# Leaving the last projection steps of a block's end to run beside the next end, in a four-layer sparse attention kernel

## The chip, the core and the metric

The kernel runs on one core of one Trainium2 chip. The metric is the device time of one execution in microseconds. The engines are called PE (matrix multiply), DVE (vector), ACT (scalar), POOL (GpSimd) and SP (the queue that issues plain DMAs). Each takes its own instructions in the order in which the program wrote them, and waits on semaphores for the others.

## What is computed

Sixteen graphs share one adjacency matrix of 1024 nodes; every node has 128 features. Four layers follow each other. Layers 0, 2 and 3 are attention over the neighbours with 8 heads, followed by a normalization, a feed-forward net of width 256 and another normalization; layer 1 is a simpler graph attention with one head. The matrix is sparse (a bit under 1 % of its entries are set), so the kernel gathers each node's neighbours instead of multiplying full matrices.

```python
# layers 0, 2, 3
Q, K, V = h @ Wq, h @ Wk, h @ Wv                # 8 heads of 16
attn = softmax(where(adj == 0, -inf, Q K^T / 4))
x = layer_norm(h + (attn @ V) @ Wo + bo)
x = layer_norm(x + relu(x @ W1 + b1) @ W2 + b2)
# layer 1
h = x @ W;  e = leaky_relu(h @ a_src + (h @ a_dst)^T)
x = layer_norm(softmax(where(adj == 0, -inf, e)) @ h + x)
```

## The kernel before

**Blocks and parts.** The work is a list of 64 blocks (`units`): 4 layers, 2 halves of 8 graphs (`g`), 8 tiles of 128 nodes (`t`). A block is gone through in parts, each of which gathers up to two chunks of neighbour rows (four in layer 1) by indirect DMAs on POOL's queue. A block of an attention layer has five parts (seven for tile 0), a block of layer 1 has three (four for tile 0). Here the five parts of a block are called A, B, C, D and E; E is the half-size mixed chunk. A prime marks the next block's parts.

**One turn of the main loop** (line 1055) handles part i in this order: `products(i)` on DVE (line 868); `summed(i-2)`, the PE sums of weighted rows (line 935); a gap; `exponentials(i)`, a DVE reduction (line 891) and an ACT exponential (line 895); a gap; `weighted(i-1)` on DVE (line 919); `gathered(i+3)`, the indirect DMAs on POOL (line 856), into one of four buffers; a gap. In layer 1 there are four gaps in a turn. The products live in four buffers, and `weighted` writes over the products of its part. A buffer is free again when `summed` has read it. Two parts that belong together are summed at once: A with B when D's turn comes, C with D in the turn of A', E in the turn of B'.

**The end of a block.** When a block's last part is summed, `divided(u)` computes the denominators on PE (the den step) and, later in the same turn, runs its second half: a DVE reciprocal (line 972), two DVE products that write `o` (line 975), an ACT copy and a POOL addition into `seen` (line 986). That point is called the closing here; it falls in the turn of the next block's part B. It creates two generators, the block's tails, one for each set of four graphs (h = 0 and h = 1). A tail is a chain of small steps:

oT (transpose of `o`, line 637), Wo (line 644), squares (line 580, ACT), power (line 586, POOL), scale (line 589, ACT), x1 (transpose, line 650), W1 with its two relus (lines 655 and 659), W2 (line 664), squares, power, scale, turn (transpose of the normalized rows, line 614), projection p0, projection p2 (line 538 on PE, line 542 on ACT), and the write of the table for the next layer (line 547, SP).

The tail of h = 1 is one step behind. The last layer has no projection: its steps after turn are a second transpose and an indirect DMA to `out` (line 625, POOL). A tail of layer 1 is shorter, because it has one normalization and no feed-forward net.

**Where the steps run.** `others()` is called in every gap. A counter (`pace`) decides whether the gap advances all tails by one step, and then one step of the next block's queries is taken (lines 799 to 832: Wq, then the replication of the queries). The rate is set at the closing: 15 steps (8 for layer 1) spread over the gaps up to the next closing. Before the second half of `divided`, all tails that are left are run to their end, `while tails: advance(tails)`. So in the kernel before, a tail always ends within one opening, the stretch from one closing to the next. With 15 steps in an opening, only the last step of h = 1, the issue of its table write, is left for that loop or the last gap.

**Buffers that tie the tails to the closing.** `o` and the normalized rows `z` share one tag with two buffers. The tile `o` of a half can only be written when the turn of the same half of the previous end has read its `z`. The small banks of PSUM (tag `ps`) are four, `yps` two.

Of the kernel before, what the change touches and what calls it, by code (L numbers as in the profile page):

```python
# [107 lines left out]

STEPS = 15
GRAPH_STEPS = 8  # L110
EDGES = 4
AHEAD = 4

# [9 lines left out]
def sparse_path(ctx: ExitStack, tc: tile.TileContext, a: dict, out: bass.AP, flag):  # L123
# [48 lines left out]
    inputs = ctx.enter_context(tc.tile_pool(name="inputs", bufs=4))  # L172
    gathers = ctx.enter_context(tc.tile_pool(name="gathers", bufs=EDGES))
    reps = ctx.enter_context(tc.tile_pool(name="reps", bufs=2))
# [7 lines left out]
    def gather_buffer():  # L182
        return gathers.tile([P, max(4 * ROW, J * (ROW + G))], F32, tag="e", name="e")
# [408 lines left out]
    def turned(z, dst, gain=None, shift=None):  # L592

        ps = bank([P, GH, P])
        for i in range(GH):
            nc.tensor.transpose(ps[:, i, :], z[:, i, :], ident)  # L596
        if gain is None:
            nc.scalar.copy(dst, ps)  # L598
        else:
            nc.scalar.activation(dst, ps, AF.Identity, bias=shift, scale=gain)  # L600
# [4 lines left out]
    def finish(l, g, t, h, z, gain, shift):  # L605
        if l + 1 < len(LAYERS):

            wanted[0] = True
            while held[0]:
                advance(slow)  # L610
            wanted[0] = False
            busy[0] += 1
            xn = states.tile([P, GH, P], F32, tag="xT", name="xT")
            turned(z, xn, gain, shift)
            yield
            yield from project(l + 1, g, t, h, xn)
            busy[0] -= 1
            return
        xn = states.tile([P, GH, P], F32, tag="xT", name="xT")
        turned(z, xn, gain, shift)  # L620
        yield
        o = twos.tile([P, GH, D], F32, tag="kv", name="outs")
        turned(xn, o)
        yield
        nc.gpsimd.indirect_dma_start(  # L625
            out=out.rearrange("n (k c) -> (n k) c", k=GR * HF),
            out_offset=bass.IndirectOffsetOnAxis(ap=places[:, g, h, t : t + 1], axis=0),
            in_=o.rearrange("p g d -> p (g d)"), in_offset=None,
        )

    def attention_tail(l, g, t, h, o):
# [38 lines left out]
        z = yield from normed(ps)  # L670
        yield
        yield from finish(l, g, t, h, z, p["ln2_g"], p["ln2_b"])

    def graph_tail(l, g, t, h, o):
# [53 lines left out]
    def at_once(g):  # L728

        spare = reps.tile([P, J, ROW], F32, tag="qr", name="spare")  # L730

        def fetch(t):
            if t < T:
                nc.sync.dma_start(
                    spare[:, t % J, :], a["x"][t * P : (t + 1) * P, columns(g, 0, HF)]
                )

        for t in range(3):
            fetch(t)
        yield  # L740
        for t in range(T):
            fetch(t + 3)
            rows = spare[:, t % J, :].rearrange("p (h g d) -> p h g d", h=HF, g=GH)
            both = []
            for h in range(HF):
                kv = None
                if h:
                    kv = exponents()[:, : 2 * GH * D].rearrange("p (c g d) -> p c g d", c=2, g=GH)
                both.append(natural(g, t, h, rows[:, h], kv))
            while both:  # L750
                advance(both)
                yield
# [5 lines left out]
    units = [(l, g, t) for l in range(len(LAYERS)) for g in range(GR) for t in range(T)]  # L758
# [10 lines left out]
    def is_attention(u):  # L769
        return LAYERS[units[u][0]][1] is ATTN  # L770
# [93 lines left out]
    def products(i):  # L864
        u, (piece,) = parts[i]
        n = len(piece)
        prs[i] = [prods.tile([P, 2, ROW], F32, tag="pr", name="pr")]
        nc.vector.tensor_tensor(  # L868
            prs[i][0][:, :n, :], es[i][:, :n, :ROW],
            qx[u].rearrange("p (o c) -> p o c", o=1) if (MIX, 0) in piece  # L870
            else of_piece(qs[u], piece),
            ALU.mult,
        )
# [114 lines left out]
    tails = []  # L988
    fronts = []
    loads = []  # L990
    slow = []

    def advance(gens):
        for gen in list(gens):
            if next(gen, "end") == "end":
                gens.remove(gen)

    pace = [0.0, 0.0]

# [17 lines left out]
    with tc.manual_schedule():  # L1017
        wide = [gather_buffer() for _ in range(EDGES)]
        setup, entry, weights = graph(wide), at_once(0), load_weights("L0")
        next(setup)  # L1020
        next(weights)
        next(entry)
        more = [weights, load_graph_weights()]
        rest = slots()
        for i, room in enumerate(setup):
            if i == T:
                for gen in more:
                    next(gen)
            if room == "load":
                for _ in loaded(0):  # L1030
                    next(entry, None)
            elif room == "queries":
                for _ in entry:
                    pass
                for _ in queries(0):
                    pass
            elif isinstance(room, str):
                next(rest)
            else:
                for _ in range(room):  # L1040
                    next(entry, None)
        for _ in entry:
            pass
        scratch.close()
        prods = ctx.enter_context(tc.tile_pool(name="prods", bufs=4))
        smalls = ctx.enter_context(tc.tile_pool(name="smalls", bufs=3))
        slow.append(at_leisure(1))
        for i in range(AHEAD - 1):
            gathered(i)
        nc.gpsimd.memset(wide[3], 0.0)  # L1050
        gathered(AHEAD - 1)
        fronts.extend([rest, loaded(1)] + more)
        closing = None
        begun = 0
        for i in range(len(parts) + 2):
            here = i < len(parts)
            u = parts[i][0] if here else len(units)
            if here:
                l = units[u][0]
                if i and parts[i - 1][0] != u:  # L1060
                    begun = i
                    if l + 1 < len(LAYERS) and LAYERS[l + 1][1] is ATTN:
                        if units[u][1:] == (0, 1):
                            more = load_weights(LAYERS[l + 1][0])
                            next(more)
                            next(more)
                        if units[u][1:] == (0, 4):
                            next(more, None)
                if is_attention(u):
                    products(i)  # L1070
            if i > 1:
                summed(i - 2)
                done = parts[i - 2][0]
                if parts[i - 1 : i] == [] or parts[i - 1][0] != done:
                    closing = divided(done)
                    next(closing)
            others()
            if here:
                exponentials(i)
            if here and i == begun + 1:  # L1080
                if is_attention(u):
                    shared(u)
                while loads:
                    advance(loads)
                if u + 1 < len(units):
                    fronts.append(queries(u + 1))
                loads.append(loaded(u + 2))
                if units[u + 2 : u + 3] and units[u + 2][0]:
                    advance(loads)
            others()  # L1090
            if 0 < i <= len(parts):
                weighted(i - 1, 0)
                if not is_attention(parts[i - 1][0]):
                    others()
                    weighted(i - 1, 2)
                gathered(i - 1 + AHEAD)
            if closing is not None and here:
                while tails:
                    advance(tails)
                for _ in closing:  # L1100
                    pass
                closing = None
                passes = 3 if is_attention(u) else 4
                steps = STEPS if is_attention(done) else GRAPH_STEPS
                pace[:] = 0.0, steps / (passes * sum(part[0] == u for part in parts) - 1)
            others()
            if i + 1 >= len(parts) or parts[i + 1][0] != u:

                while fronts:
                    advance(fronts)  # L1110
        while tails:
            advance(tails)
        for _ in closing:
            pass
        while tails:
            advance(tails)
# [434 lines left out]
```

## Time and profile before

| | |
|---|---|
| time, median of 14 runs | 2545.02 us (2532.22 to 2552.59) |
| the profiled execution | 2552.59 us, span 2550.8 us |
| mean granted PE clock | 0.909 |
| DVE busy | 1930.8 us (76 %) |
| PE busy | 2107.0 us (83 %) |
| ACT busy | 1475.2 us (58 %) |
| POOL busy | 1431.0 us (56 %) |
| start of the closings of layer 0, first and last | 190.1 us, 849.0 us |
| of layer 1 | 889.3 us, 1193.6 us |
| of layer 2 | 1240.2 us, 1846.3 us |
| of layer 3 | 1892.3 us, 2508.1 us |

The shares are means over layers with different limits, so the profile is read layer by layer and, within a layer, over one opening. A regular opening takes about 41 us in layer 0, 19 us in layer 1, 39 us in layer 2 and 41 us in layer 3. In a timeline, each row gives the start, the duration, the engine, the line, the operation, the tiles, and in brackets the idle time of that engine just before and what ended it.

### The profile page before, as it was taken

Reading aid. Unit: us, or ns where it says so; the run is one execution under the profiler, and the core shown is the slowest. Engines: PE = TensorE matmul, PEld = TensorE weight load, DVE = VectorE, ACT = ScalarE, POOL = GpSimd, SP = SyncE. Lnnn points to the kernel's source line nnn. Section 1 sums busy time; section 2 is a strip of 40 time slices with the busy share of each in tenths; the row PEclk is TensorE's granted clock in tenths of the full one; section 3 lists DMA queues with packets and bytes.
Section 4 is the critical chain, followed back from the end, with each engine's and each line's share of the span. In section 5 each row is a group of like instructions: output and inputs, shape, how many; then the busy total and the mean of one; then the engine's idle time right before and its main releaser. Section 6 shows DMA issues by size and latency. Waiting matters only on the chain. (4 is left out here: it accounts for less than half of the span.)

```text
span 2550.8 us, 36646 instructions
## 1 busy us (share of the span) xinstructions
PE 2107.0 (83%) x13124; PEld 1305.5 (51%) x13124; DVE 1930.8 (76%) x1470; ACT 1475.2 (58%) x4640; POOL 1431.0 (56%) x978
## 2 busy tenths in 40 slices
PE   6558898788887998998888888888988787788787
PEld 5425666545554554554455555655555454455444
DVE  7887787587878466676887879878797877888781
ACT  3216776566655554455476656667666565566565
POOL 3234656356665588884545546455555665665561
PEclk8679999898898999998799999999999898989898
DMA  7646888567777598897877877878777667566750
GB/s 249 236 164 225 294 289 286 208 232 251 239 253 246 167 329 317 301 340 257 277 261 247 295 260 264 276 266 287 267 259 264 238 230 264 196 231 238 244 208 19
DMA packets 168461, 636.05 MB, mean 249 GB/s; under 512 B 38328, under 2 KB 41144, under 8 KB 119774
## 3 DMA queue, kind: packets, MB, share of 16 engines
q0 software_dynamic: 92672, 485.09, 54.3%
q1 hardware_dynamic: 75600, 148.55, 17.3%
q8 instruction: 105, 1.72, 0.3%
q14 instruction: 84, 0.69, 0.1%
HBM read 603.11 MB, written 92.34 MB: 273 GB/s over the span
## 5 line engine op out<-in xcount | busy, mean ns | idle before, releaser
L856 POOL DMA_INDIRECT e<-table,idx x600 | 917.4, 1529 | 458.5 <-DVE pr L919 260.3
L919 DVE TENSOR_TENSOR pr<-e,ex 128x2048 f32<-128x2048 f32 (+1 forms) x336 | 689.6, 2060 | 203.2 <-ACT ex L895 174.8
L868 DVE TENSOR_TENSOR pr<-e,qr 128x2048 f32<-128x2048 f32 x204 | 460.9, 2259 | 180.4 <-PE acc L935 83.1
L586 POOL TENSOR_TENSOR rstd<-total,power 128x4 f32<-128x4 f32 x224 | 325.6, 1456 | 394.2 <-ACT z L580 387.0
L935 PE MATMUL acc<-pr,marks 128*32 128x512 f32 x2656 | 498.1, 620 | 39.8 <-DVE pr L919 39.3
L891 DVE TENSOR_REDUCE sc<-pr 128x128 f32<-128x2048 f32 (+1 forms) x252 | 518.5, 2058 | 8.6
L580 ACT ACTIVATE z<-yps,root 128x128 f32<-128x128 f32 x896 | 318.5, 378 | 99.6 <-PE yps L683 51.8
L596 PE MATMUL ps<-ident,z 128*128 128x128 f32 x896 | 212.6, 338 | 151.5 <-ACT z L589 151.3
L589 ACT ACTIVATE z<-yps,rstd 128x128 f32<-128x128 f32 x896 | 257.7, 383 | 92.9 <-POOL rstd L586 92.5
L596 PEld LDWEIGHTS ps<-ident,z 128*128 128x128 f32 x896 | 136.3, 159 | 335.8 <-ACT z L589 242.0
L659 ACT ACTIVATE f<-ps,b 128x512 f32<-128x512 f32 x192 | 131.9, 690 | 277.3 <-PE ps L655 277.3
L655 PE MATMUL ps<-x,W 128*128 128x512 f32 x384 | 252.0, 791 | 37.4 <-ACT x L600 37.4
L664 PE MATMUL yps<-W,f 128*128 128x128 f32 x1536 | 259.1, 286 | 17.1 <-ACT f L659 15.9
L664 PEld LDWEIGHTS yps<-W,f 128*128 128x128 f32 x1536 | 211.2, 195 | 77.7 <-ACT f L659 59.0
L935 PEld LDWEIGHTS acc<-pr,marks 128*32 128x32 f32 x2656 | 102.2, 112 | 285.3 <-issue 223.1
L538 PE MATMUL ps<-Wkv,xT 128*128 128x256 f32 x768 | 207.2, 414 | 32.4 <-ACT xT L600 27.6
L831 ACT COPY qr<-ps 128x512 f32<-128x512 f32 x384 | 197.0, 600 | 61.8 <-PE ps L828 61.8
L580 ACT ACTIVATION_READ_ACCUMULATOR z<-yps,root 128x1 f32 x896 | 194.1, 217 | 0.0
L538 PEld LDWEIGHTS ps<-Wkv,xT 128*128 128x128 f32 x768 | 146.0, 201 | 72.3 <-ACT xT L600 34.1
L542 ACT COPY kv<-ps 128x512 f32<-128x512 f32 x176 | 103.6, 589 | 134.8 <-PE ps L538 129.9
L644 PE MATMUL yps<-Wo,oT 128*128 128x128 f32 x768 | 160.7, 292 | 6.0 <-ACT oT L598 6.0
L645 PE MATMUL yps<-centre,x 128*128 128x128 f32 x768 | 158.1, 289 | 6.4
(159 smaller groups left out, 2665.5 us busy)
## 6 DMA issues: line engine op xcount, KB each, us to landing
table<-kv SPq DMA_DIRECT2D x88, 512.0 KB, 9.4
qx<-qr SPq DMA_DIRECT2D x96, 256.0 KB, 9.7
kept<-xT SPq DMA_DIRECT2D x96, 256.0 KB, 5.4
x<-kept SPq DMA_DIRECT2D x48, 512.0 KB, 10.2
e<-table,idx POOLq DMA_INDIRECT x600, 8.0
table<-kv SPq DMA_DIRECT2D x32, 256.0 KB, 10.7
edges<-in_adj SPq DMA_DIRECT2D x8, 512.0 KB, 5.1
spare<-in_x SPq DMA_DIRECT2D x8, 512.0 KB, 6.2
```

The costliest lines, as they stand in the source:

```text
L538: nc.tensor.matmul(ps[:, k, :], x[:, i + k, :], w[LAYERS[l][0], "Wkv"], start=True, stop=True,)
L580: nc.scalar.activation(z[:, i, :], y[:, i, :], AF.Square, scale=D**-0.5, bias=root, accum_out=total[:, i : i + 1],)
L586: nc.gpsimd.tensor_tensor(rstd, total, power, ALU.pow)
L589: nc.scalar.activation(z[:, i, :], y[:, i, :], AF.Copy, scale=rstd[:, i : i + 1])
L596: nc.tensor.transpose(ps[:, i, :], z[:, i, :], ident)
L655: nc.tensor.matmul(ps, p["W1"][:, f * P : (f + 1) * P], x1.rearrange("p g n -> p (g n)"), start=True, stop=True,)
L664: nc.tensor.matmul(ps[:, i, :], f1[:, f, i * P : (i + 1) * P], p["W2"][:, f, :], start=(f == 0), stop=False,)
L856: nc.gpsimd.indirect_dma_start(out=es[i][:, k, :], out_offset=None, in_=tables[l, g][:, :], in_offset=bass.IndirectOffsetOnAxis(ap=idx[:, ...
L868: nc.vector.tensor_tensor(prs[i][0][:, :n, :], es[i][:, :n, :ROW], qx[u].rearrange("p (o c) -> p o c", o=1) if (MIX, 0) in piece else of_p ...
L891: nc.vector.tensor_reduce(sc[:, :n, :], prs[i][0][:, :n, :].rearrange("p k (a d) -> p k a d", d=HD), mybir.AxisListType.X, ALU.add,)
L919: nc.vector.tensor_tensor(prs[i][k0 // 2][:, :m, :].rearrange("p k (a d) -> p k a d", d=d), es[i][:, k0 : k0 + m, base : base + ROW].rearr ...
L935: nc.tensor.matmul(outs[32 * j : 32 * j + 32], marks[:, mark, :], rhss, start=(r == 0 and chunk[0] != MIX), stop=(chunk == last),)
```

## The change

A tail now yields the word "free" once its turn step has been issued, that is, when it needs nothing more than its projection steps and its table write. At a closing only the tails that are not yet free are advanced; the others stay in the list and go on beside the tails of the block that is closed then. The number of steps in an opening is lowered by 1, 2, 3 and 2 for ends of layers 0, 1, 2 and 3, to 14, 6, 12 and 13. Tails of layer 3 never say "free", so they are still run to their end at the closing.

```diff
 STEPS = 15
 GRAPH_STEPS = 8
+
+LATE = (1, 2, 3, 2)
...
             turned(z, xn, gain, shift)
-            yield
+            yield "free"
             yield from project(l + 1, g, t, h, xn)
...
+    free = []
+
     def advance(gens):
         for gen in list(gens):
-            if next(gen, "end") == "end":
+            got = next(gen, "end")
+            if got == "end":
                 gens.remove(gen)
+            elif got == "free":
+                free.append(gen)
...
             if closing is not None and here:
-                while tails:
+                while any(gen not in free for gen in tails):
                     advance(tails)
                 for _ in closing:
                     pass
                 closing = None
                 passes = 3 if is_attention(u) else 4
                 steps = STEPS if is_attention(done) else GRAPH_STEPS
+                steps -= LATE[units[done][0]]
                 pace[:] = 0.0, steps / (passes * sum(part[0] == u for part in parts) - 1)
```

## The prediction

> **What bounds the kernel now.** I read the page's busy shares first, then the waits of DVE by layer, then the timeline of one opening, which decides. No engine is full over the span. DVE is the one whose waits are longest in the attention layers; in layer 1 it waits for gathers. This is the waits view for DVE over layer 2 (time in all, times, longest), then the busy time per engine for the three stretches of layers 1, 2 and 3.
>
> ```profile
> DVE pr L919 <- ACT ex L895: 54.3, 15, 6.3
> DVE pr L868 <- PE acc L935: 25.0, 9, 3.3
> DVE both L972 <- PE ps L935: 17.1, 6, 4.1
> ...
> core 0: us, PE busy (x) PEld busy (x) DVE busy (x) ACT busy (x) POOL busy (x), PEclk, DMA share, GB/s
> 889.00:1194.00 305.00, 276.53 (x1811) 156.68 (x1803) 202.59 (x252) 151.35 (x545) 237.56 (x180) 0.94 0.88 313
> 1240.00:1892.00 652.00, 572.36 (x3551) 357.61 (x3552) 538.48 (x309) 424.15 (x1281) 345.69 (x230) 0.94 0.78 268
> 1892.00:2474.00 582.00, 472.43 (x2989) 286.69 (x2987) 464.24 (x260) 355.87 (x1094) 352.65 (x226) 0.91 0.68 240
> ```
>
> Layer 2 leaves DVE idle for 652 − 538 = 114 us. The first two waits, 79 us, come from tail steps that stand ahead of DVE's needs in the queues of ACT and PE. The timeline of one opening of layer 2 (closing at 1403.90, next at 1443.33, so 39.4 us) shows where: DVE first, then ACT, PE and POOL.
>
> ```profile
> 1423.85 2.29 DVE L868 TENSOR_TENSOR pr<-e,qr 128x2048 f32<-128x2048 f32 x1
> 1426.17 2.29 DVE L891 TENSOR_REDUCE sc<-pr 128x128 f32<-128x2048 f32 x1
> 1432.11 1.23 DVE L919 TENSOR_TENSOR pr<-e,ex 128x1024 f32<-128x1024 f32 x1 [3.65 <-ACT ex L895]
> 1436.60 2.29 DVE L868 TENSOR_TENSOR pr<-e,qr 128x2048 f32<-128x2048 f32 x1 [3.26 <-PE acc L935]
> ...
> 1430.39 0.69 ACT L659 ACTIVATE f<-ps,b 128x512 f32<-128x512 f32 x1 [3.00 <-PE ps L655]
> 1431.25 0.69 ACT L659 ACTIVATE f<-ps,b 128x512 f32<-128x512 f32 x1 [0.17 <-PE ps L655]
> 1431.83 0.25 ACT L895 ACTIVATE ex<-sc 128x64 f32<-128x64 f32 x1
> ...
> 1420.57 1.11 PE L596 MATMUL ps<-ident,z 128*128 128x128 f32 x4 [3.17 <-ACT z L589]
> 1429.33 1.88 PE L655 MATMUL ps<-x,W 128*128 128x512 f32 x4
> 1434.64 1.92 PE L935 MATMUL acc<-pr,marks 128*32 128x512 f32 x16
> 1439.51 0.60 PE L596 MATMUL ps<-ident,z 128*128 128x128 f32 x4
> ...
> 1416.91 4.31 POOL L586 TENSOR_TENSOR rstd<-total,power 128x4 f32<-128x4 f32 x2
> 1433.63 1.04 POOL L586 TENSOR_TENSOR rstd<-total,power 128x4 f32<-128x4 f32 x1 [5.33 <-ACT z L580]
> ```
>
> The exponential of part E has its input at 1421.6, but ACT's queue holds the relus of both W1 steps before it, and those wait for PE; it runs at 1431.83, and DVE loses 3.65 us. Then the products of B' need C's buffer, and the sum of C and D (1434.64) stands on PE behind W2 of h = 1; DVE loses 3.26 us more. Together 6.91 us of 39.4.
>
> **The change, part by part.** A regular opening has 14 gaps before the closing. I wrote the steps against the gaps at the old rates (15 of 14, 8 of 11) and the new ones.
>
> *Layer 0* (14 of 14). Every step stays in its gap except the table write of h = 1, an issue on SP that goes to the first gap after the closing. Nothing on SP waits behind it but loads two blocks ahead. Zero; without that slack one issue, some 2 us, so −2 to +2 us per layer is the bound.
>
> *Layer 2* (12 of 14). The first step, oT, moves from the gap after the closing to the next one; two gaps are skipped; turn of h = 1 and p0 of h = 0 are drained just before the closing, and p2, p0, p2 and both table writes run with oT, Wo and squares of the next end. What this does:
>
> (a) E's exponential now stands before both W1 steps in ACT's queue. Its 3.65 us go: DVE reaches the products of B' at 1428.46 + 1.23 = 1429.7.
>
> (b) The PE order becomes W2 h0, W1 h1, sum of C and D, W2 h1; before, W2 h1 was ahead of the sum. W2 h1 takes 1431.13 to 1434.64, 3.5 us, so the sum ends 3.5 earlier and the products of B' start at 1433.1 instead of 1436.6. Of the 6.91 us, 3.4 remain; the gain of (a) and (b) together is 3.5.
>
> (c) A new wait: `o` of h = 1 needs turn of h = 1, now directly ahead of it. W2 h1 ends at 1433.1 + 3.5 = 1436.6. From its end to the end of turn was 1440.11 − 1434.64 = 5.5 us, so turn ends at 1442.1; the closing would be at 1443.33 − 3.5 = 1439.8 and `o` h1 at 1441.1. DVE waits 1.0 us. Behind it on DVE are the products of C, and the next oT waits too. The den step (1440.04 to 1442.29) is also PE work there, but can run while ACT scales. From 0 to 3.5.
>
> (d) In the new opening PE must do p2, p0, p2 (the same 2.9 us as after 1442.21 before) plus, first, turn, p0 and turn (0.6 + 1.1 + 0.6 = 2.3 us). Wo and the squares come some 2 us later: h0's squares ended at 1414.7, now 1416.7. Their power started only at 1416.91, held by two gathers on POOL; those gathers hide the 2 us. If that cover is gone, it costs up to 2. I take 0.
>
> (e) Less idle time on DVE leaves fewer free moments for the power steps. They take 1.04 us alone and 4.31 for a pair while DVE runs lines 919 and 868. In layer 2 the mean is 47.93 + 45.79 = 93.7 us over 64, or 1.47. I take 0.7 us more on the chain through h = 1, from 0 to 2.2 (one `weighted`).
>
> The Trainium skill, "SBUF — State Buffer", section "SBUF: two separate sides", speaks against the change here: a DVE operation with two SBUF inputs and a GpSimd one that reads SBUF exclude each other, and the one that starts second is blocked until the first is through. By that rule the last power, due when `weighted` of A' runs, would pay the full 2.2 us in every opening, and layer 2 would gain about 0.3 us per opening, 4 us in all; most powers in this trace took 1.04 us.
>
> Net per opening 3.5 − 1.0 − 0.7 = 1.8 us. Fourteen regular openings give −25 us; the ends are −49 (nothing of c to e) and +59 (all at full price: 3.5 − 3.5 − 2.0 − 2.2 = −4.2). The trace is nearest to the middle, since its gathers and its short powers are rows of the same opening. The two openings of seven parts have room (12 of 20): zero.
>
> *Layer 3* (13 of 14). All steps move one gap; no projections. E's exponential moves ahead of W2 h0 and W1 h1, but the sum of C and D still stands behind W2 h1, so the wait of DVE only moves to the products of B'. What is drained now, out h0, second transpose h1, out h1, comes after B's gather instead of before. A second `out` starts 5.8 to 10.1 us after the first (2051.25, then 2059.26). POOL waits for it with `seen`, C's gather and the powers behind. After the closing: gather 1.4, first out at 1.7, second at 9.7, `seen` (1.6) until 12.3, C's gather of two until 14.9; before, that gather ended at 2066.74, 13.6 after the closing. So 1.3 late for a power that ended 16.2 after the closing anyway. I take +0.5 us, from −1 to +2, times 14: +7 us (−14 to +28).
>
> *Layer 1* (6 of 11). POOL is the limit: 238 of 305 us busy, plus 0.3 us of issue for each of 9 gathers a block. Its order is unchanged (gather, power, power, gather). PE's three projections (2.9 us) now delay the squares; these ended at 1014.98 and their power began at 1016.73, so h0 has slack and h1's power may wait 1 us. DVE's wait for gathers covers that. Zero, with ±0.5 us times 15, ±8 us.
>
> Sum: −25 + 7 = −18 us. The profiled execution would go from 2552.6 to 2534.6; it was 7.6 us above the median of the runs, so the median goes from 2545.0 to **2527 us**.
>
> **The rivals.**
>
> *Slower: the turn of h = 1 becomes the bound at layer 2's closings.* Place: `o` of h = 1. It decides if turn ends over 4.8 us after the reciprocal, that is, if the DVE wait exceeds the 3.5 us won. For it: the chain oT to turn has 35.6 of 39.4 us already, and (d) and (e) lengthen it. Against: the gathers that hide 2 us. With a wait of 4.5 us: +1.0 × 14 + 7 = +21, 2566 us.
>
> *No difference: PE is the bound.* PE is busy 572 of 652 us in layer 2; what DVE no longer waits for E it waits for the sum, as in layer 3. The 3.5 us are eaten by (c) to (e): 2545, within 5 us. Against: PE's waits of 3.17 and 0.87 us in the same opening are room.
>
> *Larger gain: the cold PE goes too.* After the idle 3.17 us, four transposes took 1.11 instead of 0.60 us and W1 of h0 3.45 instead of 1.88 us (L655 at 1422.55 and 1429.33). If the projections fill that idle time, the chain shortens by 0.5 + 1.6 = 2.1 us, which cancels (c) and (e): −49 + 7 or better, 2490 to 2503 us.
>
> That the change does nothing holds for layer 0 alone.
>
> **How the numbers follow.** Forecast (2506 to 2539 us) 0.45; larger gain 0.16; no difference 0.13; slower 0.26. A measurement of this kernel can tell about 0.2 %, 5 us, from no change. So faster 0.61, same 0.13, slower 0.26. The range leaves out the upper part of the slower case (layer 2's full price) and the outer part of the larger gain: 2494 to 2563.
>
> **What would show it.** In layer 2: the 3.65 us wait of line 919 gone; line 868 still waiting about 3.4 us; line 975 with a new wait of about 1 us for PE line 596; closings 37.6 us apart. In layer 3: distances of 40 to 42 us as before, with the wait moved from line 919 to 868. Layers 0 and 1 within 8 us each. I am wrong if layer 3 or layer 1 moves by over 20 us, or if line 975 waits over 3 us per closing.

## The result, and the profile after

The changed kernel takes 2569.05 us (median of 10 runs, 2560.97 to 2581.76), the kernel before 2544.71 (47 runs): a ratio of 1.0099, 95% interval 1.0079 to 1.0118. It is 1 % slower; 2527 us was forecast, and the range ended at 2563. The profiled execution took 2570.18 us with a span of 2568.3; that of before, 2552.59 and 2550.8.

From the first closing of one layer to that of the next, the layers took (us, one profiled execution each; the last one ends with the span):

| | layer 0 | layer 1 | layer 2 | layer 3 |
|---|---|---|---|---|
| before | 699.2 | 351.0 | 652.1 | 658.5 |
| after | 693.5 | 371.6 | 663.6 | 646.1 |
| forecast change | 0 | 0 | −25 | +7 |
| measured change | −6 | +21 | +12 | −12 |

Executions of kernels in which a layer is unchanged scatter: layer 1 from 349 to 361, layer 2 from 646 to 652. Less than that is not read from one trace.

Layer 2, first. This is the waits view of the changed kernel for DVE over that layer, whose columns are engine, tile and line, what it waited for, us in all, times and longest:

```profile
DVE pr L870 <- DMA e<-table,idx: 50.6, 17, 4.3
DVE pr L870 <- PE acc L937: 41.7, 15, 3.6
DVE o L977 <- PE ps L598: 19.1, 12, 2.3
DVE b L488 <- PE ps L484: 7.0, 1, 7.0
DVE pr L921 <- ACT ex L897: 1.9, 1, 1.9
```

(Line numbers after stand 2 or more further down: 868 is now 870, 919 is 921, 975 is 977.) The wait for E's exponential is gone, from 54.3 to 1.9 us, as forecast. In its place stand waits for gathers, 50.6 us where it had been 4.4, longer waits for sums (25.0 to 41.7), and the new wait of `o` for the turn.

Of the layer's 11.5 us, none is in the 14 regular openings: their mean is 40.0 us in both kernels. All of it is in the two openings of seven parts, 45.9 and 46.1 us before, 52.3 and 51.4 after.

This is the timeline of the changed kernel around the opening from 1418.11 to 1460.49, by engine: DVE, POOL, ACT, PE.

```profile
1421.72 0.69 DVE L977 TENSOR_TENSOR o<-acc,both 128x512 f32<-128x512 f32 x1 [2.27 <-PE ps L598]
1439.10 1.23 DVE L870 TENSOR_TENSOR pr<-e,qx 128x1024 f32<-128x1024 f32 x1 [3.25 <-PE acc L937]
1453.76 2.29 DVE L870 TENSOR_TENSOR pr<-e,qr 128x2048 f32<-128x2048 f32 x1 [4.33 <-DMA e<-table,idx]
...
1438.18 1.03 POOL L588 TENSOR_TENSOR rstd<-total,power 128x4 f32<-128x4 f32 x1 [4.64 <-ACT z L582]
1439.57 1.62 POOL L588 TENSOR_TENSOR rstd<-total,power 128x4 f32<-128x4 f32 x1 [0.36 <-ACT z L582]
1441.63 3.09 POOL L858 DMA_INDIRECT e<-table,idx  x1 [0.44 <-DVE sc L893]
...
1429.49 0.59 ACT L600 COPY oT<-ps 128x512 f32<-128x512 f32 x1
1433.47 0.59 ACT L600 COPY oT<-ps 128x512 f32<-128x512 f32 x1 [1.61 <-PE ps L598]
1436.48 0.41 ACT L582 ACTIVATE z<-yps,root 128x128 f32<-128x128 f32 x1
...
1420.58 1.10 PE L598 MATMUL ps<-ident,z 128*128 128x128 f32 x4 [1.68 <-ACT z L591]
1421.83 3.34 PE L830 MATMUL ps<-q,rep 32*128 32x512 f32 x8
1425.11 3.78 PE L540 MATMUL ps<-Wkv,xT 128*128 128x256 f32 x8
1433.37 1.86 PE L830 MATMUL ps<-q,rep 32*128 32x512 f32 x8
1437.14 1.92 PE L937 MATMUL acc<-pr,marks 128*32 128x512 f32 x16
1441.91 3.06 PE L657 MATMUL ps<-x,W 128*128 128x512 f32 x4 [0.87 <-ACT x L602]
```

The new end's oT of h0 is copied 11.4 us after the closing and its first squares start 18.4 after it. PE has done a replication and two projections before it, at half rate (3.34 us for a replication that takes 1.86 at 1433.37; the granted clock from 1424 to 1428 is 0.50). POOL stands still for 4.64 us with the power, and the gather of D's turn, next in its queue, goes at 1441.63, 23.5 us after the closing. The sum at 1437.14, behind Wo of h1, holds the products of E for 3.25 us.

The slow stretch of PE is part of the delay. This is the changed kernel over layer 2, in the columns that the prediction shows for the kernel before:

```profile
core 0: us, PE busy (x) PEld busy (x) DVE busy (x) ACT busy (x) POOL busy (x), PEclk, DMA share, GB/s
1258.60:1922.20 663.60, 601.05 (x3556) 379.05 (x3556) 538.70 (x309) 419.28 (x1277) 370.24 (x230) 0.90 0.74 263
```

The mean granted clock fell from 0.94 to 0.90, and PE was busy 601 us where it had been 572 with practically as many matmuls. The fall is at the closings: in the first 11 us after one (mean of the 14 regular openings) the clock was 0.98 before and 0.72 after. In the opening above, half rate cost PE some 4.0 us before it reached oT. That is an estimate from rows: 0.5 on the transposes (1.10 against 0.60), 1.6 on the replication (3.34 against 1.72 at 1407.21 before), 1.9 on the two projections (3.78 against two thirds of the 2.86 that three took at 1402.79).

And there is a queue that the prediction did not follow: SP's. First the kernel before (closings at 1403.90 and 1443.33), then after.

```profile
1404.57 2.27 SPq L547 DMA_DIRECT2D table<-kv  x2
1438.51 2.81 SPq L530 DMA_DIRECT2D kept<-xT  x2
1441.49 1.15 SPq L839 DMA_DIRECT2D qx<-qr  x2
1442.68 1.25 SPq L794 DMA_DIRECT2D x<-kept  x1
```

```profile
1427.83 4.61 SPq L549 DMA_DIRECT2D table<-kv  x2
1440.40 1.14 SPq L841 DMA_DIRECT2D qx<-qr  x2
1441.59 0.59 SPq L796 DMA_DIRECT2D x<-kept  x1
1459.42 5.23 SPq L532 DMA_DIRECT2D kept<-xT  x2
```

A tail's projection begins with a store of xT to `kept`. Before, both of these stores stood on SP ahead of the copies of qx and the load of x for a later block, and held them back until 2 us before the closing. After, they stand behind: the 1 MB (2 × 256 KB and 512 KB by the page's DMA issues) leaves as soon as E's products (1439.10 to 1440.33) have read the old qx, 22 us after the closing and 1.2 us before the gather of D's turn.

Layer 1 is a matter of POOL and PE. Here is the timeline of after in the opening that begins at 1122.98 and of its block, POOL, then DVE, PE and ACT:

```profile
1123.34 0.98 POOL L858 DMA_INDIRECT e<-table,idx  x1 [4.00 <-DVE both L974]
1135.14 1.04 POOL L588 TENSOR_TENSOR rstd<-total,power 128x4 f32<-128x4 f32 x1 [3.60 <-ACT z L582]
1137.78 2.10 POOL L858 DMA_INDIRECT e<-table,idx  x1 [0.18 <-issue]
...
1118.26 0.18 DVE L902 TENSOR_TENSOR sc<-e,of 128x16 f32<-128x16 f32 x1 [4.83 <-DMA e<-table,idx]
...
1124.63 3.64 PE L937 MATMUL acc<-pr,marks 128*32 128x512 f32 x16 [7.35 <-DVE o L977]
...
1129.58 0.59 ACT L544 COPY kv<-ps 128x512 f32<-128x512 f32 x1 [6.19 <-PE ps L540]
```

In the kernel before, the two powers of an opening (here the one from 1086.36) followed on POOL without a wait, and the gather behind them went 12.4 us after the closing:

```profile
1096.53 2.06 POOL L586 TENSOR_TENSOR rstd<-total,power 128x4 f32<-128x4 f32 x2
1098.77 1.07 POOL L856 DMA_INDIRECT e<-table,idx  x1 [0.18 <-issue]
```

All three projections are behind the closing now; before, 5.9 of their 12 matmuls started there in the mean of 13 openings. PE has nothing before the closing (7.35 us idle), starts with the sums at half rate (3.64 us for what takes 1.92 at the next closing; granted clock 0.50 from 1124 to 1128), does the projections, and h0's squares end 12.1 us after the closing. POOL waits 3.60 us for them with a gather behind. Openings alternate between some 18 and 24 us; the mean of the regular ones went from 19.2 to 20.8. The gather behind the two powers goes 15.0 us after a closing in the mean, where it went at 12.5.

### The profile page after: what moved, and what is told of

It reads as the page before. It is cut to its first block, busy times and chain, and to the rows that moved or that the text cites. A ratio compares the mean times of both kernels' runs of the same rounds, so it can differ in the third digit from the quotient of the medians.

```text
span 2568.3 us, 36668 instructions
## 1 busy us (share of the span) xinstructions
PE 2141.1 (83%) x13124; PEld 1327.4 (52%) x13124; DVE 1928.2 (75%) x1470; ACT 1465.9 (57%) x4640; POOL 1423.2 (55%) x978
## 3 DMA queue, kind: packets, MB, share of 16 engines
q1 hardware_dynamic: 75600, 148.55, 17.4%
q8 instruction: 105, 1.72, 0.3%
## 5 line engine op out<-in xcount | busy, mean ns | idle before, releaser
L858 POOL DMA_INDIRECT e<-table,idx x600 | 897.3, 1495 | 493.1 <-DVE pr L921 289.0
L588 POOL TENSOR_TENSOR rstd<-total,power 128x4 f32<-128x4 f32 x224 | 338.6, 1513 | 425.4 <-ACT z L582 402.1
L598 PE MATMUL ps<-ident,z 128*128 128x128 f32 x896 | 201.7, 330 | 136.4 <-ACT z L591 136.3
L598 PEld LDWEIGHTS ps<-ident,z 128*128 128x128 f32 x896 | 128.6, 154 | 286.7 <-ACT z L591 201.5
L657 PE MATMUL ps<-x,W 128*128 128x512 f32 x384 | 231.8, 735 | 29.7 <-ACT x L602 29.7
L540 PE MATMUL ps<-Wkv,xT 128*128 128x256 f32 x768 | 237.1, 453 | 18.2 <-ACT xT L602 8.8
L833 ACT COPY qr<-ps 128x512 f32<-128x512 f32 x384 | 199.3, 599 | 45.3 <-PE ps L830 43.9
L540 PEld LDWEIGHTS ps<-Wkv,xT 128*128 128x128 f32 x768 | 160.6, 224 | 99.0 <-ACT qr L833 30.6
L830 PE MATMUL ps<-q,rep 32*128 32x512 f32 x768 | 196.1, 708 | 18.4 <-ACT q L825 15.8
L582 ACT ACTIVATION_READ_ACCUMULATOR z<-yps,root 128x1 f32 x896 | 202.7, 226 | 0.0
## 6 DMA issues: line engine op xcount, KB each, us to landing
table<-kv SPq DMA_DIRECT2D x32, 256.0 KB, 10.9
```

The source lines that it names most:

```text
L540: nc.tensor.matmul(ps[:, k, :], x[:, i + k, :], w[LAYERS[l][0], "Wkv"], start=True, stop=True,)
L582: nc.scalar.activation(z[:, i, :], y[:, i, :], AF.Square, scale=D**-0.5, bias=root, accum_out=total[:, i : i + 1],)
L588: nc.gpsimd.tensor_tensor(rstd, total, power, ALU.pow)
L657: nc.tensor.matmul(ps, p["W1"][:, f * P : (f + 1) * P], x1.rearrange("p g n -> p (g n)"), start=True, stop=True,)
L858: nc.gpsimd.indirect_dma_start(out=es[i][:, k, :], out_offset=None, in_=tables[l, g][:, :], in_offset=bass.IndirectOffsetOnAxis(ap=idx[:, ...
```

## The experiments

The table holds what the runs are read by. "Squares" is the mean time in layer 2's regular openings from a closing to the end of h0's squares; "gathers" is DVE's wait of line 868 (870 after) for them in layer 2; "clock" is PE's mean granted clock in layer 2.

| kernel | ratio to before, 95% | layer 1 | layer 2 | regular / seven parts | squares | gathers | clock |
|---|---|---|---|---|---|---|---|
| before | 1 | 351.0 | 652.1 | 40.0 / 45.9, 46.1 | 10.9 | 4.4 | 0.94 |
| after | 1.0099 [1.0079, 1.0118] | 371.6 | 663.6 | 40.0 / 52.3, 51.4 | 18.0 | 50.6 | 0.90 |
| e3 | 0.9972 [0.9946, 0.9999] | 358.9 | 646.1 | 39.7 / 45.1, 45.3 | 10.8 | 3.7 | 0.95 |
| e5 (scale fixed) | one run, 2503.36 us | 352.4 | 623.8 | 37.5 / 49.6, 49.2 | 14.4 | 46.6 | 0.96 |
| e6 (scale fixed) | one run, 2528.77 us | 352.0 | 643.1 | 39.4 / 45.9, 45.4 | 11.0 | 3.2 | 0.95 |
| e7 | 0.9875 [0.9833, 0.9916] | 351.4 | 641.5 | 38.4 / 52.0, 51.6 | 15.8 | 50.2 | 0.95 |
| e17 | 0.9838 [0.9802, 0.9874] | 344.1 | 626.8 | 38.1 / 47.0, 46.6 | 16.9 | 16.8 | 0.96 |
| e18 | 1.0081 [1.0053, 1.0108] | 374.5 | 655.8 | 39.6 / 51.2, 50.0 | 19.0 | 18.0 | 0.91 |

**Which layer (e1, e2, e3).** One number of `LATE` is set to zero, or all but the last.

```diff
-LATE = (1, 2, 3, 2)
+LATE = (1, 0, 3, 2)   # e1; e2: (1, 2, 0, 2); e3: (0, 0, 0, 2)
```

> The changed kernel with layer 1 put back (LATE = 1, 0, 3, 2: 8 steps in an opening of layer 1, nothing left over). In the two profiles the 16 openings of layer 1 took 20.6 us more than before. Theory A (leftover projections delay the squares, the power waits on POOL, the gather behind it comes late, DVE waits for the gather): layer 1 returns to 351 us within 5, the whole is about 20 us under the changed kernel, near 2549 us. Rival B (the difference between the layers is the spread of single executions): the time stays near 2569 us, within 5.

> The changed kernel with layer 2 put back (LATE = 1, 2, 0, 2). The profiles showed layer 2 slower by 11.5 us. Theory A: layer 2 returns to 652 us within 5, the whole to about 2557 us; line 977's wait for PE (19 us) and line 870's wait for gathers (51 us in layer 2) go, the wait of line 921 for the exponential (54 us) is back. Rival B: within 5 us of 2569. Rival C (the drain of the turn step ahead of the closing is what costs in layer 2): the same time as A, but then the wait at line 977 should make up most of the difference.

> Only layer 3 is changed (LATE = 0, 0, 0, 2). In the profiles layer 3 went from 658.5 to 646.1 us. If that is the effect of the later steps and of the output DMAs issued behind the gather of part B: about 2533 us, ratio 0.995. If it is the spread of single executions (rival B): 2545 us, ratio 1.000 within 0.002.

e1 took 2556.84 us, a ratio of 1.0038 [1.0014, 1.0062]; its layer 1 falls to 360.9, at the upper end of the scatter and not the 351 within 5 that had been expected; layer 2 stays at 662.4. e2: 1.0082 [1.0055, 1.0109], layer 2 back at 648.0 and its openings of seven parts at 45.8 and 45.6, layer 1 at 374.4. The whole of e2 can't be told from the changed kernel, since the two intervals overlap; layer 2's share is read from the trace alone. e3: 0.9972. So the loss is layer 1's and layer 2's, each giving up its own share in the traces when undone, and layer 3 gains. In layer 1 the gather behind the powers sorts the kernels: e1, e3, e7 and e12, where it goes 12.5 to 13.1 us after a closing, take 349 to 361 us there; e2, e4, e8 and the changed kernel, with 15.0 to 15.4, take 372 to 378 (e15, with 15.0, took 366.7).

**Power without squares (e5, e6).** In both, the power step raises a constant tile instead of the squares' total, so that the normalization has a fixed scale; e5 is the changed kernel, e6 the one before.

```diff
+    about = const.tile([P, GH], F32, name="about")
+    nc.vector.memset(about, 1.2)
...
-        nc.gpsimd.tensor_tensor(rstd, total, power, ALU.pow)
+        nc.gpsimd.tensor_tensor(rstd, about, power, ALU.pow)
```

> The changed kernel with a power step that raises a constant tile (1.2) to -0.5 instead of the sum of squares, so the normalizations scale by a fixed number and POOL never waits for ACT's squares; the power instruction itself stays. To be read against e6, the kernel before with the same edit. Theory A (POOL holds the gathers while it waits for the squares): layer 1 and layer 2 each come within 5 us of e6's. Theory F for layer 1 (copies of the leftover projections stand ahead of the exponential in ACT's queue, and their matmuls behind a sum that waits for the closing): layer 1 stays at least 10 us slower than e6's.

> The control of e5: the kernel before with the power of a constant tile. Its POOL never waits for squares either. Both theories: layers 1 and 2 at or under the kernel before, 340 to 358 us and 630 to 652 us.

With POOL, and all that follows it, free of the squares, the change is worth −25 us (2503.36 against 2528.77; one run each): layer 2 −19, layer 1 equal. Against the medians of the unedited kernels this is 66 us off the changed one (2569.05) and 16 to 23 off the other (2544.71 over all runs, 2551.43 on the same chip). So without the wait of the power behind the squares the sign turns. In layer 2 this did not go through the gathers: their 46.6 us are still there and don't come from POOL. What went in e5 are the waits behind the chain of the tails (sums from 41.7 to 14.6 us, `o` from 19.1 to 2.0). The clock came back with it (0.94 in the first 11 us after a closing, where the changed kernel had 0.72), so e5 doesn't tell the power's wait from the slow PE; each can make the other.

**The same leftovers, the first step sooner (e7, e12).** In e7 the first step of an end runs in the gap right after its closing again. The numbers in `LATE` are the same, but by the counter one step more is taken before each closing (13, 7 and 14 in a regular opening of layers 2, 1 and 3, where it was 12, 6 and 13). In layer 2 the leftovers stay the same, since the changed kernel takes that step in the drain at the closing; in layer 1 one projection is left over instead of three. So in layer 1 e7 undoes part of the change itself, not the move alone. e12 also lets the new tails step before the leftover ones.

```diff
-                pace[:] = 0.0, steps / (passes * sum(part[0] == u for part in parts) - 1)
+                rate = steps / (passes * sum(part[0] == u for part in parts) - 1)
+                pace[:] = 1.000001 - rate, rate
```

> The changed kernel with the counter started so that the first step falls into the gap right after the closing instead of the next one; rates and leftovers are the same numbers of steps, but one step more is done before each closing. In layer 1 only one projection is left, and it stands ahead of the sum that waits for the closing. Theory F: layer 1 back to 360 us or less. In layer 2 the new oT is back in its old gap: the gather wait of line 870 falls under 30 us if the one-gap shift is its cause, and stays near 50 if the leftover projections are.

> Kernel e7 with the tails of the new end stepped ahead of the leftover ones in every gap. By the theory that what counts is how soon after the closing the gather behind the powers can be issued (means in layer 2: 17.4 us before, 21.6 changed, 19.5 in e7, 20.2 with new tails first alone): that gather in layer 2 at 18.5 us or earlier and layer 2 at or under 641 us, layer 1 within 5 of 351, the whole 2515 to 2523. If the leftover copies are rather needed early (they free the small PSUM banks): slower than e7 by over 5 us.

e7: 2523.04 us beside 2551.43, close to the time that had been forecast for the change, but not by the forecast's parts: layer 2 gave 10.6 us where 25 was forecast, and layer 3, forecast at +7, gave 20. Layer 1 is at 351.4 (h0's squares end 6.0 us after a closing; 8.0 before, 10.9 after), a regular opening of layer 2 at 38.4, that is −1.6 us where −1.8 was forecast, and layer 3 at 638.3. e12 is the same within the interval (0.9898 [0.9855, 0.9941]); its gather in layer 2 came at 20.0 us, and 18.5 had been expected, a miss.

**The order in a gap, and the exponential in layer 1 (e4, e8).** e4 is the changed kernel with the new tails stepped before the leftovers. e8 lets layer 1's leftovers step only in the gap behind the exponentials, against the rival that copies of kv hold ACT.

```diff
-        for gen in list(gens):
+        for gen in sorted(gens, key=lambda gen: gen in late):   # e4
...
-            others()
+            others(True if gat else None)                        # e8
```

> The changed kernel, but in every gap the tails of the new end take their step before the leftover ones, so the new oT, Wo and squares are no longer queued behind the projections on PE and ACT. Theory A: layer 1 loses most of its 20.6 us (below 357 us) and the gather wait of line 870 in layer 2 falls from 51 us to under 35; the whole near 2550 us. Rival D (it is the shift of all steps to later gaps, not the projections in front of them): layers 1 and 2 stay within 5 us of the changed kernel's 372 and 664 us.

> The changed kernel, but in openings of layer 1 the leftover tails step only in the gap after the exponentials, once per turn, so that no copy of a leftover projection is ahead of the exponential in ACT's queue. Theory F: layer 1 falls from 372 to 378 us to 362 or less, the waits for the exponential in layer 1 from 15 to 27 us to under 10. Theory A: the squares are still behind those copies and POOL still waits, so layer 1 stays above 367 us.

e4: 1.011 [1.0075, 1.0145]; layer 2 falls to 648.9, layer 1 stays at 378.1. Neither theory fits both layers: in layer 1 the squares end no sooner for it (10.8 us after a closing), in layer 2 they end at 16.3 and the trace is shorter, though the waits for gathers stay at 50.7. e8: DVE's waits for the exponential in layer 1 fell from 14.8 to 7.5 us, layer 1 stayed at 374.0, ratio 1.0094 [1.0067, 1.0122]. That rival fell.

**Layer 0 (e11).** e7 with three leftover steps in layer 0 as well.

```diff
-LATE = (1, 2, 3, 2)
+LATE = (3, 2, 3, 2)
```

> Kernel e7 (first step in the gap right after the closing) with layer 0 given the same leftovers as layer 2 (LATE = 3, 2, 3, 2). Layer 0 stood at 694 to 701 us in all kernels so far. If what e7 showed in layer 2 (the sum of C and D ahead of W2 of h = 1, the exponential of E ahead of W1) holds there too: layer 0 down by about 9 us or more (16 openings, 0.7 us each as in layer 2), the whole near 2514 us. If layer 0's other work beside the tails (loads and transposes of its inputs) takes it back: within 5 us of e7's 2523.

1.0179 [1.0129, 1.0228]; layer 0 takes 776.8 us, 77 more, with 55 to 58 us for each of the first openings. DVE waits there for sums (79.1 us in the first five openings). Why was not tested and stays open; layer 0 also works off the input of the second half of the graphs in its idle gaps, and this is the nearest suspect.

**Layer 3's gain (e10).** The kernel before, with two idle steps ahead of a tail's output DMA, so that the gather of B's turn no longer stands behind the second of the two output DMAs on POOL. (The first is still ahead of it, by the trace some 2 us before the closing; in the changed kernel both are behind.)

```diff
+        yield
+        yield
         nc.gpsimd.indirect_dma_start(
             out=out.rearrange("n (k c) -> (n k) c", k=GR * HF),
```

> The kernel before with two empty steps ahead of the output DMA of a tail in layer 3, so that both output DMAs are issued in the drain at the closing, behind the gather of part B; all other steps keep their gaps and rates. Layer 3 took 658.5 us before and 645 to 647 us in every kernel with LATE = 2 for layer 3. If the gain of layer 3 comes from the gather of B no longer waiting behind an output DMA: layer 3 at 650 us or less, the whole near 2538 us. If it comes from the later steps (the exponential of E ahead of W2 and W1): layer 3 stays at 655 to 660 us and the whole within 5 us of the kernel before.

Layer 3 stayed at 657.9 us (658.5 before); 0.9978 [0.9958, 0.9998]. In four openings looked at, the gather went 0.2 to 1.3 us after a closing where it had gone 6.2 to 9.8 us after it (0.4 to 1.0 in the changed kernel), and nothing came of it. So the gain of layer 3 is not from that gather; it comes with the later steps, and which of them makes it was not split further.

**SP's order (e13 to e16).** In e13 (the changed kernel) and e14 (e7) the copies of qx and the load of x are issued behind the closing in layer 2, so that the first of the two kept stores is ahead of them again. e15 moves qx alone. e16 does the reverse to the kernel before.

```diff
+            hold = here and closing is not None and units[parts[i - 2][0]][0] == 2
             if here and i == begun + 1:
-                if is_attention(u):
+                if is_attention(u) and not hold:
                     shared(u)
...
-                loads.append(loaded(u + 2))
+                if not hold:
+                    loads.append(loaded(u + 2))
...
                 closing = None
+                if hold:
+                    shared(u)
+                    loads.append(loaded(u + 2))
```

> The changed kernel; at layer 2's closings the copies of qx and the load of x are issued after the closing, so that on SP they stand behind the first kept store again, as in the kernel before; nothing else moves. Theory S (SP's order: without a kept store ahead, 1 MB goes out as soon as E's products have read qx, 22 us after a closing instead of 38, among the gathers of the next parts, and these land late): DVE's waits of line 870 for gathers in layer 2 fall from 50.6 us to under 20, the two openings of seven parts go from 52 back to about 46 us, layer 2 from 664 to 640 us or less, median near 2548 us. Theory P (the gathers are late because POOL waits for the squares): these waits stay over 40 us, layer 2 stays within 5 us of 664, median near 2569.

> The kernel whose first step goes right behind the closing (2523 us, layer 2 of 641.5 us, 49 us of DVE's waits there for gathers), with SP's order of before at layer 2's closings. Theory S: these waits fall under 20 us, layer 2 to 615 to 628 us, median 2500 to 2512 us. Theory P: no change, 2523 us within 5.

> As the first, but only the copies of qx (512 KB) are issued after the closing; the load of x (512 KB) keeps its place ahead of kept. Theory S, by bytes: half of the way, waits of line 870 for gathers about 25 to 40 us, layer 2 near 652 us. If the load of x alone matters, waits as in the changed kernel (50 us); if qx alone does, as in the first of these. Theory P: no change.

> The kernel before, with the copies of qx and the load of x issued one part sooner in layer 2, ahead of both kept stores on SP, so that they go as early as in the changed kernel; no step of a tail moves. Theory S: DVE's waits for gathers in layer 2 rise from 4.4 us to 25 or more, the openings of seven parts from 46 to 50 us or more, layer 2 from 652 to about 665 us, 0.4 % slower. Theory P: nothing changes in layer 2 (652 within 4 us).

e14 holds a comparison within one trace. Its edit acted on the first opening of seven parts (from 1516.20) and, by its condition, not on the second (from 1830.71). SP's timeline in e14, in the first opening and then in the second:

```profile
1517.29 0.33 SPq L532 DMA_DIRECT2D kept<-xT  x1
1517.78 2.04 SPq L841 DMA_DIRECT2D qx<-qr  x2
1519.87 0.58 SPq L796 DMA_DIRECT2D x<-kept  x1
1562.61 0.33 SPq L532 DMA_DIRECT2D kept<-xT  x1
1563.11 0.50 SPq L841 DMA_DIRECT2D qx<-qr  x1
...
1860.97 1.14 SPq L841 DMA_DIRECT2D qx<-qr  x2
1862.16 0.95 SPq L796 DMA_DIRECT2D x<-kept  x1
1876.49 5.64 SPq L532 DMA_DIRECT2D kept<-xT  x2
```

And the waits of DVE for gathers in the same two openings:

```profile
DVE pr L870 <- DMA e<-table,idx: 1.2, 2, 1.1
...
DVE pr L870 <- DMA e<-table,idx: 6.4, 2, 3.4
```

With qx held to 1563.11 the opening takes 47.3 us and waits 1.2 for gathers; with qx out at 1860.97 it takes 51.7 and waits 6.4. The two late gathers are issued no later there (30.3 and 31.6 us after the closing in both openings, the next two at 33.2 and 34.5 against 33.9 and 35.2); they land late. e16 shows the reverse: moved early, the first takes 50.0 us and waits 6.0; not moved, the second takes 45.6 and waits 0.3. In regular openings of the kernel before, early transfers cost nothing (39.9 us); that the waits for the exponential and the sum cover them there is likely, not shown. e16 as a whole is at 1.0022 [1.0005, 1.0040]; layer 2 took 654.2 us, where about 665 had been expected, and waited 13.5 for gathers where 25 or more had been.

e14: 2520.76 us, 0.9855 [0.9815, 0.9895], where 2500 to 2512 was expected and which is not told apart from e7 by its ratio; layer 2 took 630.4 us, 11 less than in e7 and a little more than expected, and waited 23.4 for gathers (layer 0, not touched, took 712.6 in that execution). e13: 2566.24 us, 1.0043 [1.0016, 1.0070], where about 2548 was expected: gathers 27.8 us, layer 2 647.6, its openings of seven parts 50.2 and 52.7 where about 46 was expected. e15: waits 21.2, and yet layer 2 at 661.5 and 1.0072 [1.0044, 1.0099]: the waits for sums rose to 56.6.

**Both openings, and both causes (e17 to e19).** The condition now goes by the layer of the drained tails, which takes in the opening between layers 2 and 3: e17 from e14, e18 from e13; e19 is e18 with layer 1's steps given back.

```diff
-            hold = here and closing is not None and units[parts[i - 2][0]][0] == 2
+            hold = here and closing is not None and units[parts[i - 2][0] - 1][0] == 2
...
-LATE = (1, 2, 3, 2)
+LATE = (1, 0, 3, 2)   # e19 alone
```

> First step right behind the closing, and SP's order of before at every closing whose drained tails belong to layer 2, the opening between layers 2 and 3 included (it was not in the run before: 51.7 us there, with 6.4 us of waits for gathers, against 47.3 and 1.2 in the other opening of seven parts). Theory S: that opening 47 us too, layer 2 about 626 us, median 2512 to 2518 us. Theory P, or a cost of the lower rate of steps in openings of seven parts: it stays at 51 to 52 us.

> The changed kernel with SP's order of before at all those closings. Theory S: the opening between layers 2 and 3 falls from 52.7 us (51.4 in the changed kernel) to 48 to 50, where the other one already is; layer 2 about 644 us; median 2560 to 2564 us. Theory P: 52 us, 2566 us.

> The same with layer 1's two steps given back (LATE 1, 0, 3, 2): both causes taken away. If they are all that made the changed kernel slower, layer 1 is back at 352 to 361 us, layers 2 and 3 near 644 and 646 us, and the kernel is at 2530 to 2545 us, no slower than before (0.990 to 0.998). If something else still costs, it stays above before.

e17 is the fastest version, 2507.8 us beside 2548.53. Its openings of seven parts take 47.0 and 46.6 us, layer 2 takes 626.8. This is its waits view for DVE in that layer:

```profile
DVE o L977 <- PE ps L598: 29.4, 16, 2.4
DVE pr L870 <- PE acc L937: 29.0, 18, 3.4
DVE pr L870 <- DMA e<-table,idx: 16.8, 14, 3.9
```

e18 missed what was expected: 1.0081 [1.0053, 1.0108], no better than the changed kernel. Its waits for gathers fell to 18.0 us, but those for sums went to 52.9 and those of `o` to 32.1. e19 is at 0.9996 [0.9970, 1.0022], where 0.990 to 0.998 was expected: layer 1 is back at 348.7, layer 2 keeps 654.7. (Its layer 3 took 660.9 us in the profiled execution, against 645 to 649 in the other kernels with the same two steps left; one trace, not explained.) So with the chain of the tails late, gathers in time are worth little, since DVE then waits for the sums behind that chain: e15 and e18 can't be told from the changed kernel, and e13 stands 0.6 % under it. With the chain early they are worth 15 us of layer 2 by the traces (641.5 in e7 to 626.8), 10 of them in the openings of seven parts; the intervals of the two ratios overlap.

## Why the prediction was wrong

**The failed step is (d), and its counterpart in layer 1's paragraph.** It said: "Wo and the squares come some 2 us later", hidden by two gathers on POOL. Squares of h0 end 18.0 us after a closing in layer 2 where they ended at 10.9: 7.1 us later. I had counted 2.3 us of leftover PE work, at full rate. I had also written that oT "moves from the gap after the closing to the next one" and given that no price: it puts oT behind a replication and projections on PE and behind their copies on ACT, and PE ran them at half rate (some 4.0 us of the delay by the estimate above). How much of the 7.1 is the clock's and how much the new order's, no run separates. The gathers end at 14.4, so they hide 3.5 of it; the first power started at 18.3 instead of 13.0, and with it POOL's gather behind, at 21.6 instead of 17.4. e7 takes back the move (and in layer 1 two of the three leftover projections) and the change gains 1.2 %; e5 takes away the power's wait and it gains 25 us over e6, one run each. In both the clock after a closing is back (0.93 and 0.94 in layer 2). In layer 1, h0 had been given slack and h1 "1 us" that "DVE's wait for gathers covers": squares of h0 are 2.9 us later, and the wait for gathers is no cover, since what DVE waits for is issued by the POOL that stands behind those squares. It grew from 76.1 us to 91.2. Layer 1's 20.6 us are past the 20 that the prediction had named as a sign of being wrong. By luck the unforecast gain of layer 3 hid part of both misses: layers 1 and 2 together are 57 us off their forecast, the profiled execution as a whole only 36.

**"The two openings of seven parts have room (12 of 20): zero."** They lost 5.3 to 6.4 us each. I had not followed SP: the skipped steps carry kept stores, and what is queued behind a store on SP is held by it. The sentence "Nothing on SP waits behind it but loads two blocks ahead" was written for layer 0's table write and not asked again for layer 2. Here the transfers' meeting with the gathers is shown, by e14, e16 and e17. It is one of two causes: with SP's order given back and the chain late they still take 51.2 and 50.0 us (e18), with the chain early and SP as changed 52.0 and 51.6 (e7), with both given back 47.0 and 46.6 (e17).

**(a), (b), (c), (e).** E's exponential no longer holds DVE (54.3 to 1.9 us). The sum of C and D is out from behind W2 of h1, but waits for sums grew, since another sum, of A and B, now stands behind Wo of h1 (3.25 us at 1439.10). The wait of `o` for the turn was put at 1.0 us; it was 1.6 in the mean of 12. The last power of an opening, for which (e) took 0.7 us more, took 3.2 us in 8 of the 14 regular openings and 1.0 in the others; before, 1.0 in 13 of 14. In e7, whose chain is 2.2 us earlier, a regular opening gains 1.6 us against a forecast of 1.8. That is near, but no proof of the terms: e7 also waits 50.2 us for gathers, which the sum left out. Two slips carry no weight: the loop has 15 gaps before a regular closing, not 14, and 93.7 us over 64 powers is 1.46.

**Layer 3, +7 forecast, −12 measured.** The wait did move from line 919 to 868, as written: the first went from 44.8 us to almost nothing, the second's for sums from 25.8 to 50.9. But of 44.8 us only 25 came back there and 6.5 as waits for gathers (32.0 to 38.5); I had taken it one for one. POOL's order, the term that made the +7, moved nothing as far as e10 took it back.

**Layer 0** is unchanged within the scatter, as forecast.

**The rivals.** The slower rival had the place wrong: the turn of h1 costs 19.1 us in all in the changed kernel and 29.4 in e17, which is the fastest. That its 2566 us lie near the measured 2569 is luck. Against "PE is the bound" stand e7 and e17, faster with the same work on PE. A larger gain from a warm PE did not come: W1 of h0, 3.45 us in the prediction's row, still took 3.06 at 1441.91, and a second half-rate stretch came after the closing.

## What to carry to other kernels

A step moved later moves everything that stands behind it in every queue it touches: write out for PE, ACT, POOL and SP what is ahead of its first instruction in the new place, not only how many instructions were added. A store that waits in an in-order DMA queue also paces the transfers behind it; before it is moved, ask when those will go instead and what they will meet. And fixing one of two waits that run side by side can show next to nothing (e18) until the other is gone (e17).

## What the runs showed of the hardware

A transfer issued on SP slowed gathers issued on POOL: in e14's second opening of seven parts, DVE's two products waited 3.4 and 3.1 us for gathers when 1 MB went out at 1860.97, and 1.2 in all when it did not. The Trainium skill, "DMA: Bandwidth & Descriptors", section "Issuing engines are not separate DMA queues", says that transfers started by different engines run on the same 16 DMA engines and interleave; the runs agree.

The power that coincides with `weighted` (POOL in the opening from 1418.11 of the changed kernel, with DVE's line 921 from 1458.29 to 1460.57) took three times as long as one alone, and ended 0.9 us after DVE's operation:

```profile
1452.68 1.04 POOL L588 TENSOR_TENSOR rstd<-total,power 128x4 f32<-128x4 f32 x1 [2.39 <-ACT z L582]
1458.31 3.17 POOL L588 TENSOR_TENSOR rstd<-total,power 128x4 f32<-128x4 f32 x1
```

The rule of the Trainium skill that the prediction weighed ("SBUF — State Buffer", section "SBUF: two separate sides") shows here at 2.1 us. It did not decide the sign: e7, faster than the kernel before, has a power of 2.2 to 3.2 us in the second half of 12 of its 14 regular openings, as the changed kernel has (2.8 to 3.2 us in 12 of 14).

PE's granted clock went to 0.50 after idle times of quite different length. Behind 1.68 us without work (until 1420.58) the replication took 3.34 us; behind 7.35 us (until 1124.63) 16 matmuls took 3.64 instead of 1.92.
